# Three graph-attention layers and a gated graph network: two attention groups stated in pieces in turn, the first state transposed through DRAM, groups of two at both ends

## The chip, the core and the metric

The kernel runs on one core of a Trainium2 chip. A core has five engines that each work through their own instruction list: TensorE (PE: matmuls, with PEld its weight loads), VectorE (DVE), ScalarE (ACT), GpSimd (POOL) and SyncE (SP, which issues the DMAs here). They share an on-chip memory of 128 partitions (SBUF); TensorE writes its results to a second one (PSUM), from which VectorE and ScalarE fetch them. The metric is the device time of one execution in microseconds, lower is better; the time before is the median of three runs. A profile of one execution gives every instruction's start and duration.

## What is computed

There are 128 small graphs of 128 nodes with 256 features each. Three attention layers follow each other, then a gated graph network of three steps; each of the four takes the layer-normed, rectified state and adds its result to the state. All numbers are 32-bit floats. Cut to one attention layer and the last stage:

```python
h = maximum(layernorm(x), 0)                       # per node
Wh = h @ W
e = (Wh @ a1)[:, :, None] + (Wh @ a2)[:, None, :]
e = where(e > 0, e, 0.2 * e)
att = softmax(where(adj > 0, e, -9e15), axis=-1)
x = x + elu(att @ Wh)                              # layer 2: times nodemask before elu
# after three of these:
h = maximum(layernorm(x), 0)
A = (adj != 0)
for i in range(3):
    m = h @ weight[i]
    aggr = einsum('bst,bsd->btd', A, m)
    h = gru_cell(aggr, h, w_ih, w_hh, b_ih, b_hh)  # r, z: sigmoid; n: tanh
x = x + h
```

## The kernel before

**Groups.** The batch is cut into 32 groups of `G = 4` graphs (`NG = 32`). A group's tile has the 128 nodes on the partitions and 4 graphs of 256 features (or 4 adjacency matrices of 128 columns) side by side. `load(g)` (line 67) fetches x and adj of a group over SP.

**Set-up.** Before any group, the program loads the attention weights and prepares `VA` (lines 84 to 106: the weight times the two halves of `a`, so that the scores come from h directly), then the recurrence's weights: `transposed` (line 116) turns `w_hh`, `w_ih` and the three `weight[i]` on TensorE, and lines 139 to 153 form `wc[i]`, the product of `weight[i]` and `w_ih`, so that each step needs no separate message product. These use the PSUM banks of tag `gat`.

**Attention.** `attention(g, l, xt, cap)` (line 200) is a generator; its `yield`s part it into three pieces. The first takes the statistics (`stats`, line 170: VectorE for mean and variance, POOL for the power -1/2, `ve` and `rs`), the centred rectified `xn` on ScalarE, and two score vectors: `scr` on VectorE with an accumulated sum (line 212), and `pr`, a product on POOL (line 217) that ScalarE sums (line 221). The second piece transposes the second score vector to rows on TensorE (`e`, line 229), forms the masked scores `em` on VectorE, the exponential `pe` on ScalarE (line 245), and normalizes; POOL starts the output `xo` as x - 1 (line 257). The third piece transposes the attention matrix (`atp`, `at`), multiplies it with `xn` (`ahp`, `ah`, line 272), then with W (`hp`, line 285), and adds the elu to `xo` (lines 291 to 294).

**After three layers.** `gat(g)` (line 299) runs the three layers, normalizes once more into `hn` on ScalarE (line 317) and calls `turned` (line 185), which transposes `hn` on TensorE (`hTp`, eight 128x128 transposes) and copies the result to SBUF as `hT`, features on the partitions: half on ScalarE, half on VectorE.

**Recurrence.** `gru(g)` (line 324) takes `hT` as its first state `h`. Each step, for each half of the 256 features, multiplies `h` with `whh` for the three gates (`nn`, `r`, `z`, through `mm`, line 343), aggregates over the graph (`agp`, line 361, from the node-major state; from the second step on that state is a transpose of `h`, `hnp`, line 335), multiplies the aggregate `ag` with `wc[i]`, and updates the state on ScalarE and VectorE. At the end the state is transposed back, added to x in `o` and stored.

**Buffers.** Pools of 2 buffers a tag for most tiles; PSUM has 2 banks of tag `gat`, 4 of `gru`, 2 of `tr`, all of 128 x 512 floats.

**Order.** The source states whole groups, one after the other: attention of groups 0 and 1, then recurrence of group g followed by attention of group g + 2. `run` (line 422) exhausts a generator, so the `yield`s have no effect here. The source gives no order per engine; each engine's instruction list is made from the statements when the program is built, waits between engines are added there, and each engine then keeps its list. The profile shows matmuls of attention and recurrence alternating on TensorE.

Of the kernel before, what the change touches and what calls it, by code (L numbers as in the profile page):

```python
# [14 lines left out]
P = 128  # L15
# [6 lines left out]
def kernel(  # L22
# [23 lines left out]

    nc = tc.nc
# [3 lines left out]
    NG = B // G  # L51
    T = G * N
    STEPS = gweight.shape[0]
    assert N == P and B % G == 0 and B <= P and D == 2 * P and T == 512

    const = ctx.enter_context(tc.tile_pool(name="const", bufs=1))
    grp = ctx.enter_context(tc.tile_pool(name="grp", bufs=2))
    gw = ctx.enter_context(tc.tile_pool(name="gw", bufs=2))
    setup = ExitStack()
# [6 lines left out]

    def load(g):
        xt = grp.tile([P, G, D], FT, tag="x0", name=f"x_{g}")
        nc.sync.dma_start(xt, x[g * G : (g + 1) * G].rearrange("b n d -> n b d"))
        at = grp.tile([P, G, N], I32, tag="adj", name=f"adj_{g}")  # L70
        nc.sync.dma_start(at, adj[g * G : (g + 1) * G].rearrange("b i j -> i b j"))
        return xt, at

    loaded = {0: load(0)}


# [38 lines left out]

    def transposed(src, dst, nm_):
        rows = src.shape[0] // P
        t = su.tile([P, rows, D], FT, tag="wld", name=f"{nm_}_ld")
        nc.sync.dma_start(t, src.rearrange("(r p) d -> p r d", p=P))
        for k in range(KD):  # L120
            for r0 in range(0, rows, 4):
                n = min(4, rows - r0)
                ps = bank("gat", f"{nm_}_{k}_{r0}")
                for r in range(n):
                    nc.tensor.transpose(
                        ps[:, r * P : (r + 1) * P], t[:, r0 + r, k * P : (k + 1) * P], ident
                    )
                nc.vector.tensor_copy(dst[:, k, r0 * P : (r0 + n) * P], ps[:, : n * P])
# [11 lines left out]
    for i in range(STEPS):  # L140
# [3 lines left out]
        for m in range(KD):  # L144
            for o0 in range(0, O3, 384):
                ps = bank("gat", f"wcp_{i}_{m}_{o0}")
# [22 lines left out]

    def stats(xt, name):  # L170

        st = gw.tile([P, G, 6], FT, tag="st", name=f"st_{name}")
        mv = gw.tile([P, G, 2], FT, tag="mv", name=f"mv_{name}")
        for b in range(G):
            nc.vector.bn_stats(st[:, b, :], xt[:, b, :])  # L175
            nc.vector.bn_aggr(mv[:, b, :], st[:, b, :])  # L176
        nm = gw.tile([P, G], FT, tag="nm", name=f"nm_{name}")
        nc.vector.tensor_scalar(nm, mv[:, :, 0], -1.0, None, op0=OP.mult)
        ve = gw.tile([P, G], FT, tag="ve", name=f"ve_{name}")
        nc.gpsimd.tensor_scalar(ve, mv[:, :, 1], EPS, None, op0=OP.add)  # L180
        rs = gw.tile([P, G], FT, tag="rs", name=f"rs_{name}")
        nc.gpsimd.tensor_tensor(rs, ve, mhalf, op=OP.pow)  # L182
        return nm, rs

    def turned(v, pool, tag, name):

        hT = pool.tile([P, KD, T], FT, tag=tag, name=f"hT_{name}")
        for k in range(KD):
            ps = bank("gat", f"hTp_{name}_{k}")
            for b in range(G):  # L190
                nc.tensor.transpose(
                    ps[:, b * P : (b + 1) * P], v[:, b, k * P : (k + 1) * P], ident
                )
            if k % 2 == 0:
                nc.scalar.copy(hT[:, k, :], ps)
            else:
                nc.vector.tensor_copy(hT[:, k, :], ps)
        return hT

    def attention(g, l, xt, cap):  # L200

        name = f"{g}_{l}"
        nm, rs = stats(xt, name)

        xn = gw.tile([P, G, D], FT, tag="xn", name=f"xn_{name}")
        for b in range(G):
            nc.scalar.activation(xn[:, b, :], xt[:, b, :], AF.Relu, bias=nm[:, b : b + 1])  # L207

        e = gw.tile([P, 2, G], FT, tag="e", name=f"e_{name}")
        for b in range(G):  # L210
            scr = gw.tile([P, D], FT, tag="scr", name=f"scr_{name}_{b}")
            nc.vector.scalar_tensor_tensor(  # L212
                scr, xn[:, b, :], rs[:, b : b + 1], VA[l][:, 0, :], op0=OP.mult, op1=OP.mult,
                accum_out=e[:, 0, b : b + 1],
            )
        pr = gw.tile([P, G, D], FT, tag="pr", name=f"pr_{name}")
        nc.gpsimd.tensor_tensor(  # L217
            pr, xn, VA[l][:, 1 : 2, :].to_broadcast([P, G, D]), op=OP.mult
        )
        for b in range(G):  # L220
            nc.scalar.activation(  # L221
                pr[:, b, :], pr[:, b, :], AF.Copy, scale=rs[:, b : b + 1],
                accum_out=e[:, 1, b : b + 1],
            )
        yield

        e2 = bank("gat", f"e2_{name}")
        for c in range(G):
            nc.tensor.transpose(  # L229
                e2[:, c * P : (c + 1) * P], e[:, 1, c : c + 1].to_broadcast([P, P]), ident  # L230
            )

        em = gw.tile([P, G, N], FT, tag="em", name=f"em_{name}")
        for c in range(G):
            nc.vector.scalar_tensor_tensor(
                em[:, c, :], e2[:, c * P : (c + 1) * P], e[:, 0, c : c + 1], cap[:, c, :],
                op0=OP.add, op1=OP.min,
            )
        nc.vector.scalar_tensor_tensor(em, em, ALPHA, em, op0=OP.mult, op1=OP.max)
        nmx = gw.tile([P, G], FT, tag="nmx", name=f"nmx_{name}")  # L240
        nc.vector.tensor_reduce(nmx, em, axis=AX.X, op=OP.max, negate=True)  # L241
        pe = gw.tile([P, G, N], FT, tag="pe", name=f"pe_{name}")
        sm = gw.tile([P, G], FT, tag="sm", name=f"sm_{name}")
        for b in range(G):
            nc.scalar.activation(  # L245
                pe[:, b, :], em[:, b, :], AF.Exp, bias=nmx[:, b : b + 1], accum_out=sm[:, b : b + 1]
            )
        ri = gw.tile([P, G], FT, tag="ri", name=f"ri_{name}")
        nc.vector.reciprocal(ri, sm)
        if l == 2:  # L250
            nc.vector.tensor_mul(ri, ri, nmT[:, g * G : (g + 1) * G])
        nc.vector.tensor_tensor(
            pe, pe, ri.rearrange("p (g o) -> p g o", o=1).to_broadcast([P, G, N]), op=OP.mult
        )

        xo = grp.tile([P, G, D], FT, tag=f"x{l + 1}", name=f"xo_{name}", bufs=3 if l == 2 else 2)
        nc.gpsimd.tensor_scalar(xo, xt, 1.0, -1.0, op0=OP.mult, op1=OP.add)  # L257
        yield
        atp = bank("gat", f"atp_{name}")
        for b in range(G):  # L260
            nc.tensor.transpose(atp[:, b * P : (b + 1) * P], pe[:, b, :], ident)  # L261
        at = gw.tile([P, T], FT, tag="at", name=f"at_{name}")
        nc.vector.tensor_tensor(
            at.rearrange("p (g i) -> p g i", g=G), atp.rearrange("p (g i) -> p g i", g=G),
            rs.rearrange("p (g o) -> p g o", o=1).to_broadcast([P, G, N]), op=OP.mult,
        )

        ah = gw.tile([P, KD, T], FT, tag="ah", name=f"ah_{name}")
        for k in range(KD):
            ps = bank("gat", f"ahp_{name}_{k}")  # L270
            for c in range(G):
                nc.tensor.matmul(  # L272
                    ps[:, c * P : (c + 1) * P], xn[:, c, k * P : (k + 1) * P],
                    at[:, c * P : (c + 1) * P], start=True, stop=True,
                )
            if k % 2 == 0:
                nc.scalar.copy(ah[:, k, :], ps)
            else:
                nc.vector.tensor_copy(ah[:, k, :], ps)  # L279
        for j in range(G // 2):  # L280
            hp = bank("gat", f"hp_{name}_{j}")
            for b in range(2):
                c = 2 * j + b
                for k in range(KD):
                    nc.tensor.matmul(  # L285
                        hp[:, b * D : (b + 1) * D], ah[:, k, c * P : (c + 1) * P], W[l][:, k, :],
                        start=(k == 0), stop=(k == KD - 1),
                    )

            t = gw.tile([P, T], FT, tag="t", name=f"t_{name}_{j}")  # L290
            nc.scalar.activation(t, hp, AF.Exp)  # L291
            u = xo[:, 2 * j : 2 * j + 2, :].rearrange("p b d -> p (b d)")
            nc.vector.scalar_tensor_tensor(u, hp, 0.0, u, op0=OP.max, op1=OP.add)  # L293
            nc.vector.scalar_tensor_tensor(u, t, 1.0, u, op0=OP.min, op1=OP.add)  # L294
        yield xo

    done = {}

    def gat(g):
        xt, adj_t = loaded.pop(g)  # L300
        if g + 1 < NG:
            loaded[g + 1] = load(g + 1)
# [5 lines left out]
        for l in range(3):  # L308
            for v in attention(g, l, xt, cap):
                if v is not None:  # L310
                    xt = v
# [158 lines left out]
```

## Time and profile before

| | |
|---|---|
| median of 3 runs | 3126.8 us (3126.08 to 3126.9) |
| profiled execution, its own time | 3126.87 us |
| its span, first to last instruction | 3125.1 us |
| mean granted TensorE clock | 0.991 of full |
| output stores, first to last | 222.8 to 3121.2 us |
| moved by DMA | 48.03 MB, mean 15 GB/s |

The span is what the trace covers; the run's own time has a little before and after it. A row of instruction groups in the profile gives the source line, the engine, the operation, the tile written and those read (`hp<-w,ah`), the shape and the number of instructions, then busy time, the mean of one, and the idle time in front with what ended it. A 32-bit float product appears as two MATMUL records, so `x4` of 128x512 are two products. Durations of single matmuls overlap, as the next starts before the last has left the array: what one costs is read from the distance between starts.

### The profile page before, as it was taken

The numbers are of one execution on the slowest core, as the hardware profiler recorded it, in microseconds if no ns is written. First come the engines' busy times: TensorE is split into PE (matmuls) and PEld (weight loads), VectorE is DVE, ScalarE is ACT, GpSimd is POOL, SyncE is SP. The second block draws the span as 40 slices with busy tenths as digits, with TensorE's granted clock in tenths as the row PEclk, the third lists the DMA queues.
The fourth block names the chain that finished last, engine by engine and source line by source line (L and its number), as shares of the span: only waits on it lengthen the run. The fifth ranks groups of instructions, "written<-read, shape, count | busy, mean of one in ns | idle before, by whom it ended". The sixth has DMA issues, their size and how long they took to land.

```text
span 3125.1 us, 32601 instructions
## 1 busy us (share of the span) xinstructions
PE 2941.1 (94%) x11105; PEld 1714.3 (55%) x11105; DVE 2163.8 (69%) x4731; ACT 1349.4 (43%) x3265; POOL 530.0 (17%) x454
## 2 busy tenths in 40 slices
PE   5699999999999999999999999999999999999999
PEld 3455555555555555555555555555555555555554
DVE  5667776767776777776777677677667677767663
ACT  1344444444444444444444444444444444444442
POOL 1212111212111212121112121112121121111110
PEclk8899999999999999999999999999999999999999
DMA  2000000000000000000000000000000000000000
GB/s 85 11 17 11 7 18 17 17 18 11 7 18 17 18 17 11 7 17 18 17 18 11 7 17 18 18 12 13 11 18 17 17 11 7 17 14 7 8 1 14
DMA packets 56199, 48.03 MB, mean 15 GB/s; under 512 B 3296, under 2 KB 55648, under 8 KB 56032
## 3 DMA queue, kind: packets, MB, share of 16 engines
q1 hardware_dynamic: 56032, 45.95, 4.6%
q8 instruction: 87, 1.43, 0.2%
q14 instruction: 80, 0.66, 0.1%
HBM read 29.17 MB, written 16.78 MB: 15 GB/s over the span
## 4 chain that ended last, share of the span: by engine, by line
PE 70%; DVE 13%; ACT 9%; POOL 6%; issue 1%; DMA 0%; ACTq 0%; SPq 0%; POOLq 0%; DVEq 0%
PE r L344 15%; PE z L344 15%; PE ni L344 9%; PE hp L285 7%; PE nn L344 7%; PE ahp L272 6%; POOL pr L217 5%; ACT xn L207 4%; PE agp L361 3%; DVE st L175 3%; DVE xo L294 3%; DVE xo L293 3%; ACT pr L221 2%; PE hnp L335 2%; PE e L229 2%; PE atp L261 2%
## 5 line engine op out<-in xcount | busy, mean ns | idle before, releaser
L212 DVE SCALAR_TENSOR_TENSOR scr<-xn,rs,va 128x256 f32<-128x256 f32 x384 | 386.0, 1053 | 73.0 <-POOL rs L182 71.1
L344 PE MATMUL r<-ag,wc 128*128 128x512 f32 x768 | 372.1, 593 | 0.0
L344 PE MATMUL ni<-ag,wc 128*128 128x512 f32 x768 | 371.4, 592 | 0.0
L285 PE MATMUL hp<-w,ah 128*128 128x256 f32 x1536 | 368.3, 383 | 0.7 <-DVE ah L279 0.7
L344 PE MATMUL z<-ag,wc 128*128 128x512 f32 x768 | 361.4, 592 | 0.0
L257 POOL TENSOR_SCALAR xo<-xo 128x1024 f32<-128x1024 f32 x64 | 67.5, 1055 | 1596.4 <-DVE mv L176 1596.4
L285 PEld LDWEIGHTS hp<-w,ah 128*128 128x128 f32 x1536 | 284.2, 190 | 76.8 <-DVE ah L279 26.3
L293 DVE SCALAR_TENSOR_TENSOR xo<-hp,xo 128x512 f32<-128x512 f32 x192 | 131.0, 683 | 253.6 <-ACT t L291 253.6
L221 ACT ACTIVATE pr<-pr,rs 128x256 f32<-128x256 f32 x384 | 190.4, 496 | 183.5 <-POOL pr L217 183.5
L291 ACT ACTIVATE t<-hp 128x512 f32<-128x512 f32 x192 | 114.7, 597 | 353.5 <-PE hp L285 353.5
L344 PE MATMUL nn<-h,whh 128*128 128x512 f32 x512 | 261.8, 593 | 0.0
L344 PE MATMUL z<-h,whh 128*128 128x512 f32 x512 | 261.5, 592 | 0.0
L344 PE MATMUL r<-h,whh 128*128 128x512 f32 x512 | 261.5, 592 | 0.0
L392 DVE SCALAR_TENSOR_TENSOR n<-r,wn 128x512 f32<-128x512 f32 x192 | 131.4, 685 | 185.2 <-ACT r L390 185.2
L217 POOL TENSOR_TENSOR pr<-xn,va 128x1024 f32<-128x1024 f32 x96 | 236.2, 2461 | 96.6 <-ACT xn L207 96.6
L245 ACT ACTIVATE pe<-em,nmx 128x128 f32<-128x128 f32 x384 | 148.8, 389 | 209.3 <-DVE nmx L241 209.3
L361 PEld LDWEIGHTS agp<-am,hn 128*128 128x128 f32 x1536 | 204.5, 192 | 61.3 <-issue 61.0
L344 PEld LDWEIGHTS z<-ag,wc 128*128 128x128 f32 x768 | 143.3, 190 | 167.5 <-issue 167.4
L397 ACT ACTIVATE n<-n,bi 128x512 f32<-128x512 f32 x192 | 138.3, 720 | 213.1 <-DVE n L396 210.5
L390 ACT ACTIVATE r<-r,brz 128x512 f32<-128x512 f32 x192 | 131.3, 684 | 215.1 <-PE r L344 215.0
L344 PEld LDWEIGHTS ni<-ag,wc 128*128 128x128 f32 x768 | 143.5, 190 | 142.7 <-issue 132.2
L361 PE MATMUL agp<-am,hn 128*128 128x128 f32 x1536 | 218.2, 275 | 0.0
(91 smaller groups left out, 4636.6 us busy)
## 6 DMA issues: line engine op xcount, KB each, us to landing
x<-in_x_dram SPq DMA_DIRECT2D x32, 512.0 KB, 3.9
out_dram<-o SPq DMA_DIRECT2D x32, 512.0 KB, 2.9
adj<-in_adj_dram SPq DMA_DIRECT2D x32, 256.0 KB, 2.7
w<-in_L_gnn_W_dram SPq DMA_DIRECT2D x3, 256.0 KB, 6.9
ab<-in_L_gnn_a_dram SPq DMA_DIRECT2D x3, 256.0 KB, 6.6
whh_ld<-in_L_gnn_w_hh_dram SPq DMA_DIRECT2D x1, 768.0 KB, 8.4
wih_ld<-in_L_gnn_w_ih_dram SPq DMA_DIRECT2D x1, 768.0 KB, 5.9
gt_ld<-in_L_gnn_weight_dram SPq DMA_DIRECT2D x3, 256.0 KB, 2.6
```

The lines of the kernel that those rows point to most:

```text
L212: nc.vector.scalar_tensor_tensor(scr, xn[:, b, :], rs[:, b : b + 1], VA[l][:, 0, :], op0=OP.mult, op1=OP.mult, accum_out=e[:, 0, b : b + 1],)
L217: nc.gpsimd.tensor_tensor(pr, xn, VA[l][:, 1 : 2, :].to_broadcast([P, G, D]), op=OP.mult)
L221: nc.scalar.activation(pr[:, b, :], pr[:, b, :], AF.Copy, scale=rs[:, b : b + 1], accum_out=e[:, 1, b : b + 1],)
L245: nc.scalar.activation(pe[:, b, :], em[:, b, :], AF.Exp, bias=nmx[:, b : b + 1], accum_out=sm[:, b : b + 1])
L272: nc.tensor.matmul(ps[:, c * P : (c + 1) * P], xn[:, c, k * P : (k + 1) * P], at[:, c * P : (c + 1) * P], start=True, stop=True,)
L285: nc.tensor.matmul(hp[:, b * D : (b + 1) * D], ah[:, k, c * P : (c + 1) * P], W[l][:, k, :], start=(k == 0), stop=(k == KD - 1),)
L293: nc.vector.scalar_tensor_tensor(u, hp, 0.0, u, op0=OP.max, op1=OP.add)
L344: nc.tensor.matmul(ps, w[:, k, c * P : (c + 1) * P], v[k], start=start, stop=stop)
L361: nc.tensor.matmul(ps[:, b * P : (b + 1) * P], hn[k][b], am[:, b, :], start=True, stop=True)
L390: nc.scalar.activation(r, pr, AF.Tanh, bias=brz[:, cr : cr + 1], scale=0.5)
L392: nc.vector.scalar_tensor_tensor(n, r, 1.0, wn, op0=OP.add, op1=OP.mult)
L397: nc.scalar.activation(n, n, AF.Tanh, bias=bi[:, cn : cn + 1])
```

## The change

Six things are changed together.

1. **Group sizes.** `SIZES = [2, 2, 2] + [4] * 30 + [2]`: 34 groups instead of 32, the first three and the last of two graphs. `tile_of` allocates the full tile and uses the first n graphs; every loop over a group runs over n.
2. **Order of the statements.** `attention` has five pieces instead of three (a `yield` is added after `at` and after `ah`), and `gat(g)` seventeen: 3 x 5, one for the last statistics and `hn`, one for the transpose. `advance` states pieces of two groups in turn until each has a given number left. Groups 0 and 1 are stated in turn to their end; then the recurrence's weights; then group 2 until 9 pieces are left (`HALF`); then, for each g, the whole recurrence of g, and in turn the rest of group g + 2 and the first eight pieces of g + 3. `gru` is no generator any more.
3. **The recurrence's weights** are prepared after the attention of groups 0 and 1 in the source, and in the PSUM banks of tag `gru`.
4. **The first state.** `turned` is gone. VectorE transposes `hn` in blocks of 32 x 32 within each group of 32 partitions (two instructions for a group); SP stores the result to a DRAM tile and loads it back with the block rows in the other place, in four loads of 32 partitions each. `hT` now holds, per partition, for each of four blocks q of 32 nodes, the features' half, the graph and 32 nodes; `h` views it as graph, q, node, so the first step's `mm` and the first `tensor_sub` read it in runs of 32, and write or read their other operand in the same view (`like`).
5. **Within attention.** `pr` on POOL is stated ahead of VectorE's `scr`; `xo` on POOL is stated in the first piece; the exponential and the normalization work in place in `em`, and `pe` is gone.
6. **Buffers.** Two groups are loaded at the start, then g + 2 when g begins; `am` has 4 buffers instead of 3, the output tile `o` has 1.

```diff
-    NG = B // G
+    SIZES = [2, 2, 2] + [G] * ((B - 8) // G) + [2]
+    NG = len(SIZES)
+    FIRST = [sum(SIZES[:g]) for g in range(NG)]
...
+    def tile_of(pool, n, shape, tag, name, bufs=None):
+        kw = {} if bufs is None else {"bufs": bufs}
+        return pool.tile([P, G, *shape], FT, tag=tag, name=name, **kw)[:, :n]
...
-    loaded = {0: load(0)}
+    loaded = {g: load(g) for g in range(2)}
...
-    def turned(v, pool, tag, name):
...
+        pr = tile_of(gw, n, [D], "pr", f"pr_{name}")
+        nc.gpsimd.tensor_tensor(pr, xn, VA[l][:, 1:2, :].to_broadcast([P, n, D]), op=OP.mult)
+        for b in range(n):
             scr = gw.tile([P, D], FT, tag="scr", name=f"scr_{name}_{b}")
...
+        nc.gpsimd.tensor_scalar(out, xt, 1.0, -1.0, op0=OP.mult, op1=OP.add)
         yield
...
+        at = tile_of(gw, n, [N], "at", f"at_{name}")
...
+        yield
         ah = gw.tile([P, KD, T], FT, tag="ah", name=f"ah_{name}")
...
+        yield
+        for j in range(n // 2):
             hp = bank("gat", f"hp_{name}_{j}")
...
-        hT = turned(hn, grp, "h0", f"{g}_3")
+        yield
+        F = KD * n * 32
+        tr = gw.tile([P, Q, KD * G * 32], FT, tag="h3", name=f"tr_{g}_3")[:, :, :F]
+        for k in range(KD):
+            nc.vector.transpose(
+                tr.rearrange("p j (k b c) -> p k b j c", k=KD, b=n)[:, k],
+                hn[:, :, k * P : (k + 1) * P].rearrange("p b (j r) -> p b j r", j=Q),
+            )
+        d = dram.tile([Q, 32, Q, F], FT, tag=f"d{n}", name=f"d_{g}")
+        nc.sync.dma_start(d.rearrange("q r j f -> (q r) j f"), tr)
+        hT = grp.tile([P, Q, KD * G * 32], FT, tag="h0", name=f"h_{g}_0")[:, :, :F]
+        for j in range(Q):
+            nc.sync.dma_start(
+                hT[j * 32 : (j + 1) * 32], d[:, :, j, :].rearrange("q r f -> r q f")
+            )
         done[g] = (xt, am, hn, hT)
         yield
...
-        h = [h0[:, k, :] for k in range(KD)]
+        h = [
+            h0.rearrange("p q (k b c) -> p k b q c", k=KD, b=n_g)[:, k] for k in range(KD)
+        ]
...
+        def like(t, v):
+            return t.rearrange("p (b q c) -> p b q c", b=n_g, q=Q) if len(v.shape) == 4 else t
...
                 nc.tensor.matmul(
-                    ps, w[:, k, c * P : (c + 1) * P], v[k], start=start, stop=stop
+                    like(ps, v[k]), w[:, k, c * P : (c + 1) * P], v[k], start=start, stop=stop
                 )
...
-    AHEAD = 2
-    for g in range(min(AHEAD, NG)):
-        run(gat(g))
+    PIECES = 3 * 5 + 2
+    HALF = 9
+    streams = {g: gat(g) for g in range(NG)}
+    left = {g: PIECES for g in range(NG)}
+
+    def advance(*parts):
+        going = True
+        while going:
+            going = False
+            for g, keep in parts:
+                if g < NG and left[g] > keep:
+                    next(streams[g])
+                    left[g] -= 1
+                    going = True
+
+    advance((0, 0), (1, 0))
...
+    advance((2, HALF))
     for g in range(NG):
-        run(gru(g))
-        if g + AHEAD < NG:
-            run(gat(g + AHEAD))
+        gru(g)
+        advance((g + 2, 0), (g + 3, HALF))
```

## The prediction

> **What bounds the kernel now.** I read the busy shares and the slices first, then TensorE's instructions in order of time, what they waited for, and one period by itself. All sums are in the profiled execution (span 3125.1 us, itself timed 3126.87 us); the median of the three runs, 3126.8 us, lies 1.7 us above the span, and I add that at the end.
>
> ```profile
> PE 2941.1 (94%) x11105; PEld 1714.3 (55%) x11105; DVE 2163.8 (69%) x4731; ACT 1349.4 (43%) x3265; POOL 530.0 (17%) x454
> ...
> PE   5699999999999999999999999999999999999999
> ...
> PEclk8899999999999999999999999999999999999999
> ```
>
> TensorE is the bound; it is slack only at the start. The stretches show how much, and that the last stage, recurrence alone, leaves it no gap (columns: stretch, length, busy of PE, PEld, DVE, ACT, POOL, granted clock, DMA share, GB/s):
>
> ```profile
> 25.00:50.00 25.00, 19.20 (x67) 10.82 (x65) 13.31 (x29) 1.65 (x8) 0.00 (x0) 0.99 0.10 31
> 50.00:75.00 25.00, 10.43 (x40) 7.78 (x40) 13.95 (x31) 6.80 (x22) 5.76 (x5) 0.64 0.00 1
> 75.00:100.00 25.00, 11.24 (x40) 8.27 (x40) 13.54 (x33) 6.04 (x19) 4.65 (x4) 0.64 0.00 0
> 100.00:125.00 25.00, 13.10 (x53) 9.69 (x54) 13.37 (x38) 8.16 (x23) 4.98 (x5) 0.71 0.10 30
> ...
> 3075.00:3100.00 25.00, 25.00 (x77) 12.30 (x76) 8.30 (x12) 7.55 (x12) 0.00 (x0) 1.00 0.00 1
> ```
>
> The output stores come every 94.27 us (411.29, 505.55, 599.82 us). One period, between two equal transposes at 1520.36 and 1614.64:
>
> ```profile
> 1520.36:1614.64 94.28, 90.56 (x345) 52.85 (x345) 66.95 (x146) 42.11 (x103) 16.60 (x14) 1.00 0.05 15
> ```
>
> ```profile
> PE e L229 <- ACT pr L221: 3.0, 4, 1.5
> PE hTp L191 <- ACT hn L317: 1.5, 2, 0.7
> ```
>
> So 90.6 us of work and 3.7 us of waits: 3.0 for e (the two attention layers whose scores TensorE reaches about 1.3 us before ScalarE has them) and 0.74 for hTp (the window holds both its ends, hence 1.5). In the order of TensorE:
>
> ```profile
> 1520.36 0.44 PE L191 MATMUL hTp<-ident,hn 128*128 128x128 f32 x2 [0.74 <-ACT hn L317]
> 1520.64 0.39 PE L361 MATMUL agp<-am,hn 128*128 128x128 f32 x2
> 1520.86 0.43 PE L191 MATMUL hTp<-ident,hn 128*128 128x128 f32 x2
> ...
> 1564.04 0.32 PE L229 MATMUL e<-ident,e 128*128 128x128 f32 x1 [1.14 <-ACT pr L221]
> 1564.53 0.32 PE L229 MATMUL e<-ident,e 128*128 128x128 f32 x1 [0.17 <-ACT pr L221]
> ```
>
> The attention and recurrence matmuls stand mixed on TensorE although the source states whole groups one after the other. So the order in which the program states them is not the order of execution: moving statements acts through an order fixed at build time, which this trace cannot show for the changed kernel. That is the largest unknown.
>
> **The change, part by part.**
>
> *Transposes of the first state.* Removed per period: 8 hTp matmuls. A pair takes 1520.36 to 1520.64, later pairs 0.27, so 4 x 0.27 = 1.1 us of TensorE, and the 0.74 us wait in front. 31 such periods (the first group's transposes belong to the start): 31 x 1.84 = 57 us. Also removed: ScalarE's copy of hT (0.56) and VectorE's (0.68), both off the path.
>
> Added per period: two VectorE transposes of 128x512. No row has one. Below, the one-input SBUF row (cap L305, 0.43); above, for its strided sides, three such sweeps of the two-input row (0.69), 2.1 us. I take 0.69, the nearest full-width pass, so 1.4 us, net 0.7 more on an engine busy 66.95 of 94.28 us: 27 us of idle time covers it; without that cover it would be 0.7 x 31 = 22 us.
>
> Added on SP: one store and four loads per period. Issue 5 x 0.38 = 1.9 us, where SP issues three DMAs now. SP stays in order: behind the store, which waits for VectorE, and the loads, which wait for the store, stand the next input loads and the output store; inputs are wanted a period later and the output tile is free for 94 us. Round trip: store like out (2.9), four issues (1.5), load like x (3.9): 8.3 us. Today hTp ends at 1522.1 and the first matmul on hT is at 1538.4: 16 us of cover, and no TensorE time. If a 32-partition load took four times x's 3.9, the trip is 20 us and 4 us a period come out: 120 us. I take 0, as 8.3 is half the cover.
>
> [...]
>
> *First step's moving operand* is now read in runs of 32 columns, 12 products per group of four. No moving operand here is so cut. Bounds: no cost; or, as four 128-column products cost 4 x 0.111 (agp, eight in 0.89) against 0.43 for one of 512, 3.5% for three cuts, up to 17% for fifteen: 12 x 0.86 x 0.17 = 1.8 us a group, 56 us in all. I take 0: the cut here is inside one instruction, not between instructions.
>
> *Small groups.* Columns are the same in sum: 128x256 products take 0.216 (hp, fourteen in 3.02), half of 0.43. VectorE, ScalarE and SP get some fixed cost for two more groups, off the path. The last group's tail has two half-size VectorE operations and half a store: about 1 us, taken as 0.
>
> *The start.* Today the first recurrence matmul on hT is at 121.1 us: one attention of four, alone, 26 us a layer (e at 69.17 and 95.12), TensorE at clock 0.64. New: two attentions of two side by side, weight preparation (18.4 to 45.1 now) stated behind them, in other banks. Per layer some 2.1 us are fixed (ve and rs 1.3, nm, ri, hops), the rest halves: (26 - 2.1)/2 + 2.1 = 14 us for one stream; two in series 28. VectorE works 13.5 of 25 us there, so they mostly fit in each other's gaps: I take 18. First e at 17 (pr is done on ScalarE at 18.9 for four), plus 3 x 18, less 2 as the last layer ends in hn, not in e, plus 1.4 and 8.3 for the transpose through DRAM: 79 us. By then TensorE has done what it has at 121: setup and four batches of attention. Gain 42 us; with 14 it is 54, with 28 it is 12. Behind it two small groups (35 us each) are ready at once and cover the next attentions.
>
> *Two streams in turn.* The work is unchanged; what can change is the 3.0 us of e. I keep it: the order is planned as before, attention stated ahead of the next recurrence, and what makes ScalarE late (POOL's pr at 2.46 us, then four sums) is unchanged. Bounds: all of it goes, -3.0 x 31 = -93; or it doubles, +93. In-place exp, the earlier xo on POOL and the loads two ahead cost nothing: POOL is busy 17 of 94 us and loads land in 4.
>
> Sum: 3125.1 - 57 - 42 = 3026; plus 1.7 for the median: **3028 us**.
>
> **Rivals.**
>
> *The e waits go as well.* For: two chains give twice the work to fill in, and the recurrence alone leaves no gap (25.00 of 25.00). Against: TensorE did have other work at 1564, and was still sent to e too early. 3028 - 93 = 2935.
>
> *Only the start gains.* As many new waits (1.84 us a period) come as go: 3028 + 57 = 3085. For it: a wait that ends at TensorE often reappears at the next operand.
>
> *Collisions, slower.* POOL's pr and VectorE's sums get in each other's way:
>
> ```profile
> 1560.66 0.49 DVE L212 SCALAR_TENSOR_TENSOR scr<-xn,rs,va 128x256 f32<-128x256 f32 x1 [0.93 <-POOL rs L182]
> ...
> 1561.07 2.56 DVE L212 SCALAR_TENSOR_TENSOR scr<-xn,rs,va 128x256 f32<-128x256 f32 x1
> ```
>
> ```profile
> 1560.90 2.45 POOL L217 TENSOR_TENSOR pr<-xn,va 128x1024 f32<-128x1024 f32 x1 [0.28 <-ACT xn L207]
> ```
>
> The same operation takes 0.49, and 2.56 while pr runs: 2.1 us of VectorE per pr. Now only one attention is in flight, and it is at the sums itself. With two, the other stands in its em, at or ah, operations that TensorE waits for directly. Three pr a period; if two meet the other stream: 4.2 x 31 = 130, so 3028 + 130 = 3158. It decides from 99/31 = 3.2 us a period. Against: VectorE idles 27 us a period, and the recurrence covers late attention. [...]
>
> *It does not do what it says:* the planned order hardly follows the new statements. The start still gains from the smaller groups, and the transposes leave TensorE; that is the forecast again.
>
> **How the numbers follow.** Forecast (2975 to 3075, its own range from the start's ends 12 and 54 and a third of the e bounds) 0.55; e waits gone 0.15; only the start 0.10; collisions or a late state, slower, 0.17; near zero by cancelling 0.03. What this kernel's measurement tells from no change is about 0.2%, 6 us. Faster 0.80, same 0.03, slower 0.17. Range: down to 2925 (e gone and 10 more from the start), up to 3130, where the slower cases start; these leave out most of the 0.17 and little else.
>
> **What would show it.** Output stores 92.4 us apart (89.4 if the e waits go, 95 or more if collisions win); no transposes of hn on TensorE; first matmul on the state near 79 us; POOL-to-ScalarE waits of e about 3 us a period; loads of the state landing over 5 us before their first use. Wrong: new TensorE waits for at, ah or em over 1 us each, products of the first step longer than 592 ns, or the first recurrence after 100 us.

## The result, and the profile after

The changed kernel takes **3201.97 us** (median of 4 runs, 3200.64 to 3203.64) against 3126.85 us before in the same comparison: ratio 1.0239, 95% interval 1.0221 to 1.0257. It is slower by 75 us where 99 us of gain were forecast. The profiled execution has a span of 3201.8 us at a mean granted clock of 0.979 (before 0.991).

Busy time and slices of the changed kernel, from its page:

```profile
PE 2986.6 (93%) x11137; PEld 1739.4 (54%) x11137; DVE 2180.4 (68%) x4897; ACT 1336.9 (42%) x3295; POOL 528.0 (16%) x482
...
PE   6788999999999999999999999999999999999999
...
PEclk9899999999999999999999999999999999999999
```

The shares are nearly those of before. The slices differ at the start, where TensorE fills sooner but has a dip before it is full. The stretches show that dip (columns: stretch, length, busy of PE, PEld, DVE, ACT, POOL, granted clock, DMA share, GB/s):

```profile
75.00:100.00 25.00, 13.87 (x51) 11.16 (x51) 12.97 (x41) 6.89 (x18) 4.20 (x7) 0.64 0.22 64
100.00:125.00 25.00, 20.81 (x105) 17.57 (x104) 18.02 (x51) 13.43 (x38) 8.13 (x8) 0.99 0.06 22
...
150.00:175.00 25.00, 19.80 (x105) 16.02 (x104) 21.74 (x55) 12.32 (x36) 7.04 (x6) 0.95 0.04 10
```

From 150 to 175 us, where the forecast had small recurrences covering the next attentions, TensorE is busy for 19.80 of 25 us and VectorE for 21.74. The output stores say what that cost: 4 graphs are out at 207.0 us (before 222.8), but 16 graphs at 523.8 (halfway between the stores of 14 and of 18; before 505.6). Sixteen microseconds of lead have become 18 of delay before the steady part begins.

There the stores are 97.06 us apart (mean of the 19 distances from the ninth store on; before 94.30). One period, between equal points, with its two halves of different kind ahead of it:

```profile
1541.00:1600.00 59.00, 53.22 (x225) 32.27 (x224) 51.57 (x125) 30.13 (x84) 16.30 (x14) 1.00 0.13 41
1600.00:1637.00 37.00, 37.00 (x111) 18.49 (x110) 15.05 (x24) 11.30 (x17) 0.00 (x0) 1.00 0.00 1
1543.85:1640.32 96.47, 90.69 (x338) 51.16 (x337) 67.09 (x149) 41.43 (x101) 16.30 (x14) 1.00 0.08 25
```

The attention of both streams stands in the first 59 us, where VectorE is busy for 51.57; in the other 37 GpSimd has nothing to do and TensorE no gap. Averaged, VectorE still idles 29 us of 96. TensorE's waits in that period (seconds column: us in total, times, longest):

```profile
PE e L173 <- ACT pr L163: 4.0, 4, 3.0
PE atp L201 <- DVE mv L134: 1.1, 1, 1.1
PE hp L227 <- DVE ah L220: 0.5, 1, 0.5
PE agp L330 <- ACT hn L321: 0.2, 1, 0.2
```

The wait for hTp is gone, with its transposes. The waits for e have grown from 3.0 to 4.0 us, one of them alone 3.0, and three waits are new. The longest, on TensorE, then what VectorE and GpSimd did ahead of it:

```profile
1577.12 0.40 PE L173 MATMUL e<-ident,e 128*128 128x128 f32 x2 [3.03 <-ACT pr L163]
```

```profile
1568.60 0.17 DVE L134 BATCH_NORM_AGGREGATE mv<-st 128x2 f32<-128x6 f32 x1
1568.72 0.43 DVE L133 BATCH_NORM_STATS2 st<-xo 128x6 f32<-128x256 f32 x1
1569.06 0.67 DVE L220 COPY ah<-ahp 128x512 f32<-128x512 f32 x1
...
1572.21 0.48 DVE L158 SCALAR_TENSOR_TENSOR scr<-xn,rs,va 128x256 f32<-128x256 f32 x1
...
1572.62 2.56 DVE L158 SCALAR_TENSOR_TENSOR scr<-xn,rs,va 128x256 f32<-128x256 f32 x1
```

```profile
1572.37 2.53 POOL L155 TENSOR_TENSOR pr<-xn,va 128x1024 f32<-128x1024 f32 x1 [0.60 <-ACT xn L151]
```

The ah copy of one stream stands among the statistics of the other, and a scr that takes 0.48 us takes 2.56 beside pr. ScalarE sums pr only when GpSimd has it, so e is late, and behind the long scr VectorE holds the other stream's work back.

The clock adds to the waits. Between 500 and 2900 us the granted clock is at half for 68.3 us in all in the changed kernel, each time from a point where TensorE had stood waiting for 2 us or more of the last 3.41, and never in the kernel before. At half clock four products of 128x512 in a row took 3.50 us (at 1384.18), at full clock 1.88 (at 1387.51). By this some 34 of the 75 us are TensorE's work at half speed (an estimate: half of the 68.3 us).

### The profile page after: what moved, and what is told of

Same layout as the page of the kernel before. It is cut to its first block, busy times and chain, and to the rows that moved or that the text cites. A ratio compares the mean times of both kernels' runs of the same rounds, so it can differ in the third digit from the quotient of the medians.

```text
span 3201.8 us, 33247 instructions
## 1 busy us (share of the span) xinstructions
PE 2986.6 (93%) x11137; PEld 1739.4 (54%) x11137; DVE 2180.4 (68%) x4897; ACT 1336.9 (42%) x3295; POOL 528.0 (16%) x482
## 4 chain that ended last, share of the span: by engine, by line
PE 62%; DVE 14%; ACT 13%; POOL 8%; issue 3%; DMA 0%; SPq 0%; ACTq 0%; DVEq 0%; POOLq 0%
PE r L313 16%; PE z L313 15%; PE ni L313 8%; PE nn L313 8%; POOL pr L155 6%; PE hp L227 4%; ACT xn L151 4%; PE agp L330 4%; ACT pr L163 3%; DVE st L133 3%; PE ahp L213 2%; DVE xo L236 2%; DVE xo L235 2%; ACT em L188 2%; PE hnp L304 2%
## 5 line engine op out<-in xcount | busy, mean ns | idle before, releaser
L158 DVE SCALAR_TENSOR_TENSOR scr<-xn,rs,va 128x256 f32<-128x256 f32 x384 | 379.6, 1040 | 48.5 <-POOL rs L140 44.2
L313 PE MATMUL r<-ag,wc 128*128 128x512 f32 (+1 forms) x816 | 401.5, 595 | 3.9 <-DVE ag L334 3.9
L313 PE MATMUL ni<-ag,wc 128*128 128x512 f32 (+1 forms) x816 | 395.5, 595 | 4.9 <-DVE ag L334 3.9
L313 PE MATMUL nn<-h,whh 128*128 128x512 f32 (+1 forms) x816 | 398.9, 571 | 0.0
L313 PE MATMUL r<-h,whh 128*128 128x512 f32 (+1 forms) x816 | 397.3, 568 | 0.0
L313 PE MATMUL z<-h,whh 128*128 128x512 f32 (+1 forms) x816 | 397.2, 568 | 0.0
L313 PE MATMUL z<-ag,wc 128*128 128x512 f32 (+1 forms) x816 | 370.2, 569 | 0.0
L155 POOL TENSOR_TENSOR pr<-xn,va 128x1024 f32<-128x1024 f32 (+1 forms) x102 | 246.1, 2413 | 139.4 <-ACT xn L151 136.0
L313 PEld LDWEIGHTS z<-h,whh 128*128 128x128 f32 x816 | 154.8, 191 | 162.8 <-issue 144.0
L365 ACT ACTIVATE n<-n,bi 128x512 f32<-128x512 f32 (+1 forms) x204 | 141.6, 694 | 219.8 <-DVE n L364 219.7
L313 PEld LDWEIGHTS r<-h,whh 128*128 128x128 f32 x816 | 151.2, 191 | 147.7 <-issue 144.5
```

Of the source, the lines that this page charges most:

```text
L155: nc.gpsimd.tensor_tensor(pr, xn, VA[l][:, 1:2, :].to_broadcast([P, n, D]), op=OP.mult)
L158: nc.vector.scalar_tensor_tensor(scr, xn[:, b, :], rs[:, b : b + 1], VA[l][:, 0, :], op0=OP.mult, op1=OP.mult, accum_out=e[:, 0, b : b + 1],)
L313: nc.tensor.matmul(like(ps, v[k]), w[:, k, c * P : (c + 1) * P], v[k], start=start, stop=stop)
L365: nc.scalar.activation(n, n, AF.Tanh, bias=bi[:, cn : cn + 1])
```

## The experiments

All times are medians. "Period" is the mean distance of output stores in the steady part (the 19 from the ninth store on), "16 graphs" the time when that many are stored; with three groups of two no store ends at 16, and it is the point halfway between the stores of 14 and of 18. The ratio is to the kernel before, run beside it.

| run | what it is | us | ratio, 95% | period | 16 graphs |
|---|---|---|---|---|---|
| | before | 3126.85 | | 94.30 | 505.6 |
| | after | 3201.97 | 1.0221 to 1.0257 | 97.06 | 523.8 |
| t1 | before, DRAM transposes only | 3122.7 | 0.9969 to 0.9991 | 93.50 | 523.9 |
| t2 | after, one stream, whole groups | 3119.3 | 0.9958 to 0.9981 | 93.46 | 524.1 |
| t3 | after, all groups of four | 3202.4 | 1.0205 to 1.0264 | 96.85 | 530.8 |
| t4 | after, TensorE transposes | 3271.0 | 1.0414 to 1.0493 | 99.95 | 522.2 |
| t5 | one stream, spaced | 3173.5 | 1.0126 to 1.0156 | 95.54 | 545.6 |
| t6 | t5, all groups of four | 3158.3 | 1.0077 to 1.0109 | 95.95 | 525.3 |
| t7 | after, its two streams spaced | 3117.7 | 0.9946 to 0.9975 | 93.94 | 542.6 |
| t8 | t5, two small groups, first | 3163.9 | 1.0093 to 1.0123 | 95.62 | 532.8 |
| t9 | after, pr on VectorE | 3064.7 | 0.9781 to 0.9810 | 92.79 | 497.5 |
| t10 | before, pr on VectorE | 3141.3 | 1.0024 to 1.0052 | 95.01 | 500.0 |
| t11 | t6 in another order | 3062.8 | 0.9771 to 0.9801 | 92.14 | 514.1 |
| t12 | t10, DRAM from third group | 3102.1 | 0.9897 to 0.9927 | 93.93 | 497.8 |
| t13 | t9, and pr still made by GpSimd | 3277.6 | 1.0458 to 1.0493 | 99.54 | 534.7 |
| t14 | t2, pr on VectorE | 3115.4 | 0.9943 to 0.9973 | 93.92 | 509.3 |
| t15 | t11, pr on VectorE | 2991.1 | 0.9546 to 0.9574 | 90.04 | 497.8 |
| t16 | t15, the change's sizes | 3004.8 | 0.9591 to 0.9619 | 90.03 | 514.4 |
| t17 | t15, first two groups turned on TensorE | **2983.0** | 0.9516 to 0.9545 | 90.06 | 490.0 |
| t18 | t15, all groups turned on TensorE | 3018.9 | 0.9630 to 0.9662 | 91.26 | 492.8 |

### One part of the change at a time (t1 to t4)

The kernel before with the transposes through DRAM alone, the edit of the change in `gat` and `gru` and nothing else of it:

> The kernel before with one part of the change alone: the first state is transposed by VectorE in blocks and through DRAM, everything else as before (groups of four, whole groups stated one after the other). If the transposes through DRAM are as cheap as forecast, output stores come 92.4 us apart (94.27 less 1.1 of transposes and 0.74 of wait) and the time is about 3127 - 57 = 3070 us. If they are what made the changed kernel slow, stores come about 97 us apart and the time is 3200 or more.

The other way round, the changed kernel with the statements of before:

```
-    advance((2, HALF))
     for g in range(NG):
         gru(g)
-        advance((g + 2, 0), (g + 3, HALF))
+        advance((g + 2, 0))
```

> The changed kernel with the attention stated by whole groups again after each recurrence (groups 0 and 1 are still stated in turn); transposes through DRAM, small groups and all else stay. If the two streams in turn are the cause (waits for e, atp and hp that grew, and the clock that drops in them), stores come about 92.4 us apart instead of 97.1 and the time falls by some 28 x 4.7 = 130 us to about 3070. If the cause lies in another part, it stays within 20 us of 3202.

Its sizes undone (`SIZES = [G] * (B // G)`), and its transposes undone (the eight TensorE transposes and two copies of `turned` in place of the DRAM trip):

> The changed kernel with 32 groups of four. The changed kernel passed its tenth graph 14 us later than the kernel before, where 42 us earlier was forecast. If the small groups are why (their 35 us recurrences are too short to cover the attention behind them), this one gains at the start: 10 to 40 us, 3160 to 3190. If the start was slow for another reason (the two attentions in turn, the late weights), it is at 3202 or above, since two attentions of four take longer than two of two.

> The changed kernel with the first state's transposes back on TensorE, all else as changed. If they cost TensorE 1.1 us a group and a wait, as read from the kernel before, stores come 98 to 99 us apart and the time is 3225 to 3265. If the way through DRAM is what hurts, the time falls towards 3127.

t2 names the part at fault: with whole groups stated in turn the period is 93.46 and all of the loss is gone. The two interleaved streams cost 3202 - 3119 = 83 us. t3 clears the small groups of the loss (3202.4 against 3202.0); in this order they even have 16 graphs out 7 us sooner. t4 shows that the DRAM trip pays inside the change, 69 us, more than in t1, where it gains some 6 (ratio 0.998). Not all of the 69 us is TensorE's work: the granted clock is at half for 112.6 us between 500 and 2900 us in t4, against 68.3, which is some 22 us (an estimate: half of the difference). In t1 the period falls by 0.8 us, not 1.84: a new wait of 0.6 us takes the place of hTp's 0.74, and 0.4 us stay unexplained. TensorE's waits in t1, whole run:

```profile
PE e L231 <- ACT pr L223: 102.1, 128, 8.5
...
PE z L365 <- DVE n L417: 16.6, 29, 0.6
```

The rest of its gain is given back once, at the start: the first product on the state starts at 141.4 us instead of 121.1, and 16 graphs are out 18 us later than before. In t2 and in the changed kernel they are as late, though other parts of the start differ there.

### Streams stated with recurrence pieces between them (t5 to t8)

If e is waited for because it is stated right behind what makes it, recurrence pieces between the two should cure it. `gru` yields six pieces a step (G), the attention of the group two ahead five a layer (a):

```
-    advance((2, HALF))
+    ORDER = "aGGGaGaGaGa" * 3 + "aa"
     for g in range(NG):
-        gru(g)
-        advance((g + 2, 0), (g + 3, HALF))
+        rec = gru(g)
+        for what in ORDER:
+            if what == "G": next(rec)
+            elif g + 2 < NG: next(streams[g + 2])
+        for _ in rec: pass
```

> The kernel after with one attention stream, its pieces stated between pieces of the recurrence (six a step), so that three recurrence pieces (about 11 us of matmuls) stand ahead of each e; the whole computation is kept. Theory: the e waits come from e being stated right behind the instructions that make its operand, so with matmuls stated between them they fall from 4.2 us a period to under 0.5, the period from 97.0 to about 90, the time to about 2995 us (2970 to 3030). Rival, that the chain t, stats, pr, scr is late however it is stated: period 93 or more, time near the 3119 of the single stream.

> The same with 32 groups of four. Steady part as in the run before (period about 90). If the small groups cost time at the start, because 35 us of recurrence cannot hide an attention of more, this is the faster of the two by 15 to 40 us; if the early start of the recurrence is a gain, the slower by 20 to 40.

The same spacing with both streams of the change (b is the group three ahead), `ORDER = "aGbG" * 8 + "aGG"`:

> The kernel after with its two streams (groups g+2 and g+3) and its small groups kept, but each attention piece followed by a recurrence piece. If the loss came from how closely the pieces are stated (bunching), the e, atp and hp waits go as with one spaced stream: period about 90, time 2980 to 3030. If two streams collide on VectorE, GpSimd and ScalarE however they are spaced, the period stays at 95 or more, time 3130 to 3200.

And t5 with two small groups, both at the start, and no small last one:

> The one spaced stream with two groups of two ahead and 31 groups of four, no small last group. Same period as the first run. Tells whether the third small group and the small last group matter: within 10 us of the first if they do not; 20 to 35 us slower if the small last group shortens the tail.

t5 is a miss that teaches. The waits for e do go, but the time falls by 29 us only, not by the 207 expected: in a period of it TensorE waits for one thing only (first its waits, then VectorE's instructions ahead of such a wait in the order of time).

```profile
PE r L313 <- DVE ag L334: 4.9, 3, 2.3
```

```profile
1518.98 0.69 DVE L334 COPY ag<-agp 128x512 f32<-128x512 f32 x1
1519.58 2.07 DVE L158 SCALAR_TENSOR_TENSOR scr<-xn,rs,va 128x256 f32<-128x256 f32 x1
...
1522.40 0.68 DVE L334 COPY ag<-agp 128x512 f32<-128x512 f32 x1
```

The second ag copy of the recurrence is queued behind three of the four scr, one of them held by pr. So the wait had moved from attention to recurrence. t7 says that two streams do not collide as such: spaced out, the change's own two streams and sizes run at 93.94 and 3117.7 us. What costs the 83 us, with pr on GpSimd as it is here, is that both streams' pieces follow each other with nothing between. The small groups are a loss here: 15 us against groups of four (t6), 10 of them saved with two in place of four (t8); at 16 graphs t5 lies 20 us behind t6 and 13 behind t8.

### The row products taken off GpSimd (t9, t10, t12 to t14)

The one edit, in each kernel:

```
-        nc.gpsimd.tensor_tensor(pr, xn, VA[l][:, 1:2, :]..., op=OP.mult)
-        for b in range(n):
-            scr = ...; nc.vector.scalar_tensor_tensor(scr, xn[:, b, :], rs[:, b : b + 1],
-                VA[l][:, 0, :], ..., accum_out=e[:, 0, b : b + 1])
-        for b in range(n):
-            nc.scalar.activation(pr[:, b, :], ..., accum_out=e[:, 1, b : b + 1])
+        for j in (1, 0):
+            for b in range(n):
+                scr = ...; nc.vector.scalar_tensor_tensor(scr, xn[:, b, :], rs[:, b : b + 1],
+                    VA[l][:, j, :], ..., accum_out=e[:, j, b : b + 1])
```

> The kernel after with the row products pr, so far one multiply on GpSimd and four passes of ScalarE a layer, made by VectorE in the same form as scr; the computation is kept. In the trace one scr in four takes 2.56 instead of 0.48 us, the one beside pr. Theory: in this stage GpSimd's pr holds VectorE up for 2.06 us a layer and lengthens the chain in front of e; without it VectorE's total stays (215 us more of work, 198 us less of holding), ScalarE loses 260 us, and the e waits fall by 1 to 2 us each: period 97.0 to 95 or 96, time 3140 to 3180. Rival, that the pr holding is no part of the loss: period 97, 3190 to 3210.

> The kernel before with the same single edit. Its e wait of 2.97 us a period should fall to about 1 or 1.5: period 94.27 to 92.5 or 93, time 3065 to 3090. If pr is hidden anyway: 3127.

t9 is the largest single finding. One edit takes 137 us from the changed kernel and makes it faster than before by 2.05% (interval 1.9 to 2.2). VectorE gets 384 more products, yet its time in scr falls: 768 products take 346.2 us where 384 had taken 379.6. The period falls by 4.27 us, the granted clock is never at half between 500 and 2900 us, and e is now waited for once a period, for 1.2 us:

```profile
PE e L167 <- DVE xo L229: 1.2, 1, 1.2
PE ahp L207 <- DVE at L197: 0.8, 1, 0.8
PE atp L195 <- DVE em L189: 0.6, 1, 0.6
```

t10 was expected to gain and is 12 us slower than before. Its waits fell as expected (e from 2.97 to 1.77 us a period), but two close together now cost the clock. Both waits, then the stretches around them:

```profile
805.68 0.29 PE L221 MATMUL e<-ident,e 128*128 128x128 f32 x1 [0.98 <-DVE scr L213]
806.76 0.32 PE L221 MATMUL e<-ident,e 128*128 128x128 f32 x1 [0.79 <-DVE scr L213]
```

```profile
803.00:807.00 4.00, 2.23 (x7) 0.76 (x7) 3.07 (x8) 2.28 (x5) 3.06 (x3) 1.00 0.00 0
807.00:811.00 4.00, 4.00 (x9) 1.60 (x9) 3.29 (x16) 0.00 (x0) 0.00 (x0) 0.57 0.01 2
811.00:815.00 4.00, 4.00 (x11) 1.85 (x10) 3.02 (x7) 1.11 (x4) 0.00 (x0) 1.00 0.00 0
```

Four microseconds at a granted 0.57 cost 1.7 us, and the periods of t10 come in two lengths, 95.63 and 93.94, which differ by just that. Without the dip it would be a third of a microsecond faster than before, no more.

t9 removes two things: GpSimd's hold on VectorE (the scr of 2.56 us beside a pr), and the chain through GpSimd and ScalarE ahead of e. t13 puts back the first alone: GpSimd makes pr as well, and nothing reads it.

```
+        nc.gpsimd.tensor_tensor(pr, xn, VA[l][:, 1:2, :]..., op=OP.mult)
         for j in (1, 0):
```

> The kernel after with both rows of products made by VectorE, and GpSimd's multiply pr kept beside them, its result unused. The chain in front of e is then the short one, and VectorE is held as before. If the 4.2 us a period that went with pr were the holding of VectorE: period back at 96 to 99, time 3170 to 3260. If they were the chain alone (pr 2.5 us and four ScalarE passes ahead of e): period 93 to 94, time 3065 to 3105.

It costs 213 us, 6.75 a period. The scr rows of t13 and of t9, over the whole run (busy, mean ns):

```profile
L159 DVE SCALAR_TENSOR_TENSOR scr<-xn,rs,va 128x256 f32<-128x256 f32 x768 | 545.0, 766 | 77.0 <-POOL rs L140 74.5 <-ACT xn L151 2.3
```

```profile
L157 DVE SCALAR_TENSOR_TENSOR scr<-xn,rs,va 128x256 f32<-128x256 f32 x768 | 346.2, 509 | 76.6 <-POOL rs L140 72.8 <-ACT xn L151 3.2
```

The same 768 instructions take 199 us longer beside a product that nothing reads, and the kernel 213, though VectorE is idle for over a quarter of it. The two numbers are near each other, but the 213 hold some 22 us of clock as well (at half for 88.5 us in t13, 45.0 in t9). A rival is GpSimd's own queue, with rs late behind pr; but VectorE waits for rs ahead of scr about as long as in t9 (74.5 and 72.8 us). So the hold alone is enough for the loss. What the longer chain adds in the changed kernel was not separated from it.

> The kernel after with one attention stream, stated whole, and pr on VectorE. If the change's interleaved pieces are worth something once pr no longer holds VectorE, this stays 30 to 60 us above the interleaved version with the same edit (3064.7), at 3095 to 3125 and a period of 93 or more; if pr alone was the matter, both are within 10 us.

With whole groups stated (t14) the same edit is worth 4 us, which the two intervals do not tell from nothing. Hence the interleaved pieces are worth 3115 - 3065 = 50 us once pr is off GpSimd, and cost 83 while it is on it. Each edit alone misleads; they have to be tried together.

The kernel before with pr on VectorE, and with the trip through DRAM from the third group on:

```
-        hT = turned(hn, grp, "h0", f"{g}_3")
+        if g < 2:
+            hT = turned(hn, grp, "h0", f"{g}_3")
+        else:
...
```

> The kernel before, with the DRAM transposes from the third group on (the first two groups keep the TensorE transposes) and with pr on VectorE. Theory: the DRAM trip costs 18 us once, at the start, where no recurrence hides it (16 graphs are out at 523.9 instead of 505.6 in every version with it), and saves 0.8 us a group after; so with its start unchanged it gains 0.8 x 30 = 24 us on the run with pr alone. Rival, that the start loss has another cause: no gain on the run with pr alone.

t12 is faster than t10 by 39 us, expected 24: 2 us of it are in hand at 16 graphs, the rest comes in the periods, 95.01 to 93.93, partly because fewer of them have the dip (41.0 us at half clock between 500 and 2900 us, 61.4 in t10: some 10 us of time).

### The order that leaves no wait (t11, t15 to t18)

In t11 the piece with the statistics and scr is stated behind the recurrence piece that has the ag copies, `"GaGGGaGaaGa" * 3 + "aa"`, with 32 groups of four:

> One spaced stream, 32 groups of four, the pieces in another order: the attention piece that fills VectorE with stats and scr is stated behind the recurrence piece with the ag copies instead of ahead of it. Theory: what replaced the e wait in the spaced streams (r waits for ag, 4.2 us a period) is VectorE's queue order alone: both waits go, period 90 to 91.5, time 3000 to 3050. Rival, that the same VectorE time has to be waited for somewhere: period 93 to 95, time 3090 to 3150.

> One spaced stream in the second order, 32 groups of four, and pr on VectorE. Its only wait was atp, 2.1 us a period: with the e chain shorter and the holding gone the period should be 90 to 91 (88.7 of matmuls and about 1.3 around them), time 2985 to 3030. If VectorE's total is what is waited for, 92 as before, 3060.

> The same with the change's sizes (three groups of two, thirty of four, one of two). With pr gone after's small groups had 16 graphs out at 497.5 us, 8 ahead of before; so this should have them out 10 to 20 us sooner than the run with groups of four, and end 10 to 20 us sooner. If small groups cannot cover the attentions next to them, it ends 5 to 20 us later.

t11 against t6 is the statement order alone: 95 us. Both waits went, but a new one of 2.1 us for atp came, so it ended above its forecast of 3050. With pr on VectorE as well (t15) that goes too. A period of t15, and TensorE's one wait in it:

```profile
1488.25:1578.28 90.03, 89.71 (x337) 51.84 (x336) 66.29 (x171) 35.65 (x77) 8.40 (x11) 1.00 0.08 27
```

```profile
PE ahp L207 <- DVE at L197: 0.2, 1, 0.2
```

This is TensorE's own work, with nothing left to gain from waits. t16 then shows the small groups by themselves in this order: 16.6 us lost by 16 graphs, 13.7 at the end.

The last two runs price the trip through DRAM in the same schedule, with TensorE transposes under `if g < 2` (t17) and in every group (t18):

> The fastest version so far (one spaced stream, second order, groups of four, pr on VectorE) with the first two groups' transposes on TensorE and the DRAM trip from the third on. Theory: the trip is uncovered for the first group only, 10 to 18 us there; the first output moves from 227.6 to 210 or 218 and the end from 2991 to 2973 or 2982. Rival, that the trip is hidden there too: 2988 to 2993.

> The same version with TensorE transposes in all groups, so that the only difference to 2991 is the change's trip through DRAM. In this schedule TensorE waits 0.2 us a period, so what the transposes cost it shows whole: the forecast's 1.1 us of transposes and 0.7 us of waiting for hn a period would make the period 91.1 to 91.9 and the time, less 10 to 18 us at the start, 3010 to 3035. If VectorE's transposes cost as much as they free, 2991.

From t18 to t17, 36 us in 30 groups, 1.2 us a period: that is what leaving TensorE is worth. From t17 to t15, 8 us: that is the trip of the first group, which nothing hides (the first store comes at 227.6 instead of 219.9 us). t17, at 2983.0 us, is 4.7% faster than before (interval 4.55 to 4.84) and beats both kernels.

## Why the prediction was wrong

The forecast was 3028, the median is 3202, 174 too little. By the output stores: the forecast has 16 graphs out at 505.6 - 42 - 3 x 1.84 = 458 us, the kernel at 523.8, so 66 us went by then. From 16 to 120 graphs the kernel takes 2519.9 us, and 26 periods of 92.43 would be 2403: 117 more. The last 8 graphs take 155.0, some 5 less than forecast.

- *Two streams in turn, 0 us.* This step failed: "I keep it: the order is planned as before". From 572 to 2515 us, twenty periods of 97.15 us where 92.43 were forecast, the waits for e are 4.0 us a period instead of 3.0, new waits of atp, hp and agp are 1.1, and the granted clock, for which the forecast has no term here, is at half for 58.0 us in all, which costs 1.45 us a period (an estimate: half of it, by twenty). That is 3.6 of the 4.7 us; the rest is not traced to a row. What makes ScalarE late was indeed unchanged, but what stands between had changed: pieces of two attentions, with nothing of the recurrence between them (t2, t7).
- *The rival that came true is the one of collisions.* Its mechanism, pr holding VectorE while the other stream's at and ah stand behind, agrees with the runs: without pr the period falls by 4.27 us (t9). That its price, two of three pr or 4.2 us, is so near is in part luck: it was reckoned as time of VectorE on top of the 92.43, while the trace shows it as longer waits of TensorE and as lost clock, and in t9 waits that were there before have gone as well. It was given 0.17, "against: VectorE idles 27 us a period". That was an average. In the 59 us where both attentions run VectorE is 87% busy.
- *Two of three pr.* The rival's price counted two of the three pr of a period. All three, at the 2.1 us of the forecast's own rows, are 6.3 us; with GpSimd's product put back in t13 the period is 6.75 us longer than in t9, clock included. In the changed kernel a scr beside a pr of 2.53 us took 2.56, about as long as the pr; in the kernel before it was 2.56 beside 2.45. By what GpSimd slows VectorE, no run shows.
- *The start, +42 us of gain.* It is a loss of 18 by 16 graphs. First e at 17.3 as forecast, a layer takes 23 us instead of 18, the first product on the state starts at 96.9 instead of 79. So 24 of the 42 us were there. The step that failed next is that two small groups "are ready at once and cover the next attentions": they do not (TensorE is busy for 19.80 of 25 us from 150 us on). But small groups alone don't explain the 66 us: in this order groups of four are 7 us later still (t3), the small ones cost 16.6 us only in the order of t16, and taking pr off GpSimd brings 16 graphs forward by 26 us (t9). How the rest divides stays open.
- *Transposes, -57 us.* Direction right, too large: 36 where it can be seen alone (t18 to t17), since 1.2 us a period come out and not 1.84. In the kernel before, with a new wait in their place, 0.8 (t1); in the changed kernel 2.9 (t4), part of it clock.
- *The trip through DRAM, 0 us.* Right in the steady part: store 2.6 and loads 4.2 us to landing, inside the cover. Wrong for the first group, where too little runs beside it: 8 us (t17 to t15), and in the kernel before 18 by 16 graphs (t1).
- *VectorE's transposes* took 0.686 us each, 0.69 forecast.
- *First step's moving operand, 0 us.* Right: from 600 to 2500 us every product of the state with whh, of the first step and of the later ones, takes 592 to 595 ns in the changed kernel.

## What to carry to other kernels

Read how busy an engine is in the stretch where the moved work will stand, not over the period: 27 us of idle time were no cover, since they lay where nothing needed them. Before two streams are interleaved, look for an instruction that takes five times its usual time beside another engine (here scr, 2.56 us instead of 0.48) and remove that pair first; the same reordering was worth +83 us with it and -50 without. And when a wait is cured by moving statements, look at whose queue the moved pieces now stand ahead of, as the recurrence's ag copies behind scr show.

## What the runs showed of the hardware

The granted clock fell at short waits. In the changed kernel it is at half from 1380.60 to 1387.43 us, around the end of a wait of 3.04 us at 1381.59 (the same columns as above):

```profile
1376.00:1381.00 5.00, 2.56 (x10) 1.52 (x8) 4.72 (x9) 2.84 (x10) 3.87 (x3) 0.96 0.00 0
1381.00:1386.00 5.00, 4.41 (x9) 2.27 (x10) 4.33 (x13) 1.65 (x4) 0.00 (x0) 0.50 0.01 2
1386.00:1391.00 5.00, 5.00 (x15) 2.32 (x14) 4.52 (x15) 1.57 (x5) 1.65 (x2) 0.86 0.00 0
```

In t10 two waits of 0.98 and 0.79 us with 0.29 us of work between them were enough, while single waits of 1.49 us (before) and 2.07 us (t11) left it at 1.00, and a like wait of 3.03 us at 1577.12 in the changed kernel did so too. The clock's records part these cases. In the traces of before and after they hold full and half only, and change (9 and 53 times) only at points that lie a whole number of 3.41 us apart. In t10, with the fall at 807.48, both waits lie in the one stretch of that length ahead of it:

```profile
804.07:807.48 3.41, 1.64 (x6) 0.62 (x5) 2.48 (x8) 1.71 (x4) 2.07 (x2) 1.00 0.00 0
807.48:810.90 3.42, 3.42 (x7) 1.34 (x6) 2.71 (x13) 0.00 (x0) 0.00 (x0) 0.50 0.01 2
```

In the changed kernel the wait at 1381.59 leaves its first stretch busy for 1.37 us and the clock falls; the one at 1577.12 is shared by two stretches, and it doesn't:

```profile
1377.19:1380.60 3.41, 1.37 (x5) 0.48 (x3) 3.41 (x3) 1.25 (x6) 3.29 (x2) 1.00 0.00 0
1571.75:1575.16 3.41, 2.33 (x9) 1.33 (x7) 3.36 (x7) 1.25 (x4) 2.72 (x3) 1.00 0.00 0
1575.16:1578.57 3.41, 1.46 (x7) 0.95 (x8) 3.34 (x10) 2.48 (x10) 0.93 (x1) 1.00 0.00 0
```

Between 500 and 2900 us the clock falls 16 times in the changed kernel, each time behind a stretch in which TensorE was busy for at most 1.39 of 3.41 us, and never behind one with 1.40 or more. In t10 it falls 18 times, behind 1.64 or 1.65, and once not behind 1.64; the kernel before has no stretch under 1.75 and no fall. So in the changed kernel the falls go with TensorE's busy time in such a stretch, and not with the length of a wait: 3.04 us with a fall, 3.03 without. No one busy time divides the runs: in t7 the clock falls behind 1.97 to 2.03 us and not behind one of 1.94, in t4 behind up to 1.80 and not behind one of 1.49.

In the changed kernel a scr beside GpSimd's pr took 2.56 us instead of 0.48, and in t13 the scr took 766 ns on the mean instead of 509 (t9), though nothing read GpSimd's product. Reading the moving operand in runs of 32 columns cost no time: 592 to 595 ns a product in the changed kernel, and the same in the kernel before.
